# A per-token factor turned by VectorE and DMA instead of TensorE, in a Strassen-Winograd matmul chain

## The chip, the cores and the metric

The kernel runs on one core of a Trainium2 chip. The metric is the device time of one execution in microseconds (us). The engines of the core are TensorE (PE, with its weight loads listed apart as PEld), VectorE (DVE), ScalarE (ACT), GpSimd (POOL) and SyncE (SP, which here only issues DMAs). Everything is fp32.

## The reference, cut to what matters

x holds 8 batch rows of 256 tokens with 1024 features. Two layers follow each other, each added to its own input:

```
logits = x @ Wr.T + 5 * onehot(language of the row)          # 8 experts
w      = softmax(top 2 of logits);  gates = w at those two, 0 elsewhere
h      = x @ A.T                                              # 8 experts x 16 ranks = 128 numbers a token
x1     = x + x @ W.T + 2 * sum_e gates[e] * (h[e] @ B[e].T)   # W is 1024 x 1024
out    = x1 + x1 @ weight[adapter of the row].T               # 1024 x 1024, one of 16 by row
```

So per token there is a vector of 128 gated numbers, `gates * h`, and the last term of x1 is that vector times a 128 x 1024 matrix ("up projection").

## The kernel before, in words

**Layout.** Features lie on partitions, tokens along the free axis. The 2048 tokens are two halves j of 1024 and four quarters of 512. The product x @ W is done by Strassen-Winograd: seven products of 512 x 512 x 1024 blocks in place of eight, and most of these have two or three "leaves" that are split into seven again. The second layer (`adapt`, lines 896 to 1006) does the same per batch row with the row's weight; it comes after and takes from 226 us to the end.

**The first layer's order** is written out in lines 1031 to 1096: `opening` (product "1", mixed with the down projection of half 0), then the down projection of half 1 (`project`, lines 1037 and 1043), then `product` "2", "5", "6", "3", "7", "4". Products 2, 5, 3 and 4 also carry the up projection: `mm` (line 549) appends, after a block's own matmuls, one step per output half `ms` with `up[rows]` as stationary and `hg[tokens]` as moving operand (line 554). A step is two matmul instructions of 512 columns; four products with four such pairs of steps give 64 instructions. Product 2 and 4 read half 0 (`hg[0]`), 5 and 3 half 1.

**The gated numbers.** `project` leaves h and the logits in PSUM with tokens on partitions. `take` (line 265) adds the bias to the logits on DVE and copies h to `hT[j]` (128 tokens x 8 chunks x 128) on ACT. `gating(j)` (line 290) is a list of 20 small DVE operations (one on ACT), and at its end `onto_h`, which multiplies `hT[j]` by the gates (128 x 1024). The up projection needs the 128 numbers on partitions and tokens along the free axis, so `turn(j, banks)` (line 323) does 8 transposes of 128 x 128 on TensorE against the identity, and two ACT copies into `hg[j]`; the copy for j = 1 also changes the sign. `turn(0)` is called at line 1046, between the last `project` and product 2; `turn(1)` inside product 2 at its line 761 (`between`).

**What sets the order.** Each engine runs its instructions in program order; PE's order is written by hand. DVE's order is made at build time by a planner: it keeps a running time for PE and DVE (`now`), costs each DVE operation at (columns + 66)/960 us, and holds optional operations in `queue` as (cost, events to wait for, key, function). Before each DVE operation that empties a PSUM bank (`after`, line 394), `ahead` (line 366) issues from the queue what is ready and fits before PE gets there; `force(key)` (line 383) issues what PE is about to need. The chip itself waits by semaphores only. So an operation that is later than the planner thought delays what stands behind it on DVE, and PE where it needs that.

**Around the change.** Product 2 (line 693 on, key "2", leaves 2 and 4) starts with a block product into bank A, then ACT copies A to bank X (line 720), then come leaf 2's first piece into `single0` ("P" in the profile), block B5 (`t1`, `s1`) with its up step, leaf 2's piece 5 into `single1`, and a second block product that accumulates onto A. `single0` and `single1` hold the last down projection until `take(1, 1)` has emptied them; A must have been copied to X. On POOL's queue, `add_x` (line 1017) adds x blocks with DMAs into "12" and "22": those are inputs of products 5 and 6. On SP's queue, `raw("21", 0, 1)` (line 1065) follows product 2.

Of the kernel before, what the change touches and what calls it, by code (L numbers as in the profile page):

```python
# [9 lines left out]
F32 = mybir.dt.float32  # L10
I32 = mybir.dt.int32
AF = mybir.ActivationFunctionType
ALU = mybir.AluOpType
# [3 lines left out]
P = 128  # L17
NE = 8
LANG_BIAS = 5.0
SCALING = 2.0  # L20
# [5 lines left out]
def kernel(  # L26
# [62 lines left out]
    def flat(blk):  # L89
        return blk.rearrange("p k n -> p (k n)")  # L90
# [32 lines left out]

    aw_sb = flat(yb["12"])[:, : KC * EA].rearrange("p (k e) -> p k e", k=KC)
    hT = [flat(yb["22"])[:, j * C * ER : (j + 1) * C * ER].rearrange("p (c e) -> p c e", c=C) for j in range(2)]

    small = {}

# [92 lines left out]
    def copy(out_, x, scale=1.0):  # L221
        if scale == 1.0:
            nc.scalar.copy(out_, x)
        else:
            nc.scalar.activation(out_, x, AF.Copy, scale=scale)  # L225
# [13 lines left out]
        add(d, d, ident.unsqueeze(1).to_broadcast([P, k1 - k0, P]))  # L239


    hg = [const.tile([ER, 2, TQ], F32, name=f"hg{j}") for j in range(2)]
    lg = [rtile([P, C, E], f"lg{j}") for j in range(2)]
    gate8 = {}

# [43 lines left out]

    def gating(j):  # L290

        m1, hot1, ops1 = first_max(lg[j], j, 1)
        rest = rtile([P, C, E], "rest")
        m2, hot2, ops2 = first_max(rest, j, 2)
        dm = rtile([P, C], "dm")
        ex = rtile([P, C], "ex")
        den = rtile([P, C], "den")
        g1 = rtile([P, C], "g1")
        g2 = rtile([P, C], "g2")
        wide = [P, C, E]  # L300

        def onto_h():
            h = hT[j].rearrange("p c (e r) -> p (c e) r", r=R)
            g = hot1.rearrange("p c e -> p (c e)").unsqueeze(2).to_broadcast([P, C * E, R])
            tt(h, h, g, ALU.mult)


        ops = ops1 + [
            lambda: nc.vector.scalar_tensor_tensor(rest, hot1, NEG, lg[j], ALU.mult, ALU.add)
        ] + ops2 + [  # L310
            lambda: minus(dm, m2, m1),
            lambda: nc.scalar.activation(ex, dm, AF.Exp),
            lambda: nc.vector.tensor_scalar(den, ex, 1.0, None, ALU.add),
            lambda: nc.vector.reciprocal(g1, den),
            lambda: nc.vector.tensor_scalar(g1, g1, SCALING, None, ALU.mult),
            lambda: tt(g2, g1, ex, ALU.mult),
            lambda: tt(hot1, hot1, g1.unsqueeze(2).to_broadcast(wide), ALU.mult),
            lambda: tt(hot2, hot2, g2.unsqueeze(2).to_broadcast(wide), ALU.mult),
            lambda: add(hot1, hot1, hot2),
        ]  # L320
        return [(0.26, f) for f in ops] + [(us(2 * TQ), onto_h)]

    def turn(j, banks):

        for n in range(C):
            nc.tensor.transpose(banks[n // CQ][:, ts(n % CQ, P)], hT[j][:, n, :], ident)  # L326
        for c, ps_g in enumerate(banks):
            copy(hg[j][:, c, :], ps_g, -1.0 if j else 1.0)


    bdiff = const.tile([ER, OG + 3 * OQ], F32, name="bdiff")
# [19 lines left out]
    def us(n):  # L351
        return (n + 66) / 960

    def vec(t, fn, key=None):
        fn()
        now["dve"] += t
        done[key] = now["dve"] + 0.1

    def event(name, later=0.0):
        events[name] = now["pe"] + later  # L360
# [56 lines left out]
    def third(key, leaf, lhs, rhs, place, what):  # L417

        ra = lambda i, j: lhs()[:, j, ts(i, P)]
        rb = lambda i, j: rhs()[:, i, ts(j, NQ)]
        n0, n1 = slice(0, NQ), slice(NQ, TQ)
        t, own = {}, {}
        at = {"r13": 0, "r2": P, "r4": 2 * P, "q13": 3 * P, "q2": 3 * P + NQ, "q4": 3 * P + 2 * NQ}
        me = f"{key}:L{leaf}"

        def op(name, tag, fn, x, y, what):
            width = P if name[0] == "r" else NQ

            def run():
                if place == 0:
                    t[name] = sub3.tile([P, width], F32, name=f"{name}_{key}{leaf}", tag=tag)
                elif place == 3:
                    t[name] = flat(yb["12"])[:, 2048 + at[tag] : 2048 + at[tag] + width]
                else:
                    t[name] = spare(1536 + (place - 1) * 1152 + at[tag], width)
                fn(t[name], *(t[v] if isinstance(v, str) else v() for v in (x, y)))

            return us(width), what, f"{me}.{name}", run  # L440

        A, B = (lambda i, j: lambda: ra(i, j)), (lambda i, j: lambda: rb(i, j))
        ops = [
            op("r1", "r13", add, A(1, 0), A(1, 1), what),
            op("q1", "q13", minus, B(0, 1), B(0, 0), what),
            op("r2", "r2", minus, "r1", A(0, 0), what),
            op("q2", "q2", minus, B(1, 1), "q1", what),
            op("r4", "r4", minus, A(0, 1), "r2", what),
            op("q4", "q4", minus, B(1, 0), "q2", what),
        ]  # L450
        ops3 = [
            op("r3", "r13", minus, A(0, 0), A(1, 0), (f"{me}.5",)),
            op("q3", "q13", minus, B(1, 1), B(0, 1), (f"{me}.5",)),
        ]

        def piece(n, acc=None, banks=None, fresh=False):
            if n in (1, 5):
                own[n] = (single(f"P{n}_{key}{leaf}", n // 5) if banks is None else banks[n // 5])[:, n0]
            for x in {3: ("r4",), 4: ("q4",), 5: ("r1", "q1"), 6: ("r2", "q2", "P1"), 7: ("r3", "q3", "P6")}.get(n, ()):
                force(f"{me}.{x}")  # L460
            out_, l, r = {
                1: lambda: (own[1], ra(0, 0), rb(0, 0)),
                2: lambda: (acc[:, 0, n0], ra(0, 1), rb(1, 0)),
                3: lambda: (acc[:, 0, n1], t["r4"], rb(1, 1)),
                4: lambda: (acc[:, 1, n0], ra(1, 1), t["q4"]),
                5: lambda: (own[5], t["r1"], t["q1"]),
                6: lambda: (own[1], t["r2"], t["q2"]),
                7: lambda: (own[1], t["r3"], t["q3"]),
            }[n]()
            nc.tensor.matmul(out_, lhsT=l, rhs=r, start=(n in (1, 5) or fresh and n in (2, 4)), stop=True, skip_group_check=True)  # L470
            now["pe"] += 0.432
            event(f"{me}.{n}", 0.2)

        def take(n, dest, base=None, sub=False):

            cut = lambda v: {1: v[:, 0, n0], 6: v[:, 0, n1], 5: v[:, :, n1]}[n]
            if n == 7:
                cut = lambda v: v[:, 1, :].rearrange("p (j n) -> p j n", j=2)
            src = own[5 if n == 5 else 1]
            if n in (5, 7):  # L480
                src = src.unsqueeze(1).to_broadcast([P, 2, NQ])
            evict(NQ if n in (1, 6) else TQ, cut(dest), src, None if base is None else cut(base), f"{me}.P{n}", sub)

        return ops, ops3, piece, take
# [61 lines left out]
    def multiply(up=None, tokens=None):  # L546


        def mm(acc, lhs, rhs, first=False, rows=None, c=0, part=(0, 1), ms=(0, 1), need=()):
# [1 line left out]
                force(key)  # L551
            steps = [(lhs[:, k, ts(m, P)], rhs[:, k, :], m) for k in part for m in ms] if part else []
            if up is not None and rows is not None:
                steps += [(up[rows][:, ts(m, P)], hg[tokens][:, c, :], m) for m in ms]
            for i, (l, r, m) in enumerate(steps):
                nc.tensor.matmul(  # L556
                    acc[:, m, :],
# [132 lines left out]
        out(5, q2, q2)  # L690
        add(q2, A, q2)

    def product(key, base, dest, lora=None, tokens=None, sub=False, joined=None, between=None):

# [16 lines left out]
        own = list(deep[2][1]) if 2 in deep else []  # L713
        own += late[:1] + (deep[3][0] if 3 in deep else []) + late[1:] + (deep[4][0] if 4 in deep else [])
        own += (deep[3][1] if 3 in deep else []) + (deep[4][1] if 4 in deep else [])
        queue[:0] = own
        A = new("A")
        mm(A, a(0, 0), b(0, 0), True)
        X = new("X")
        nc.scalar.copy(X, A)  # L720
        if 2 in deep:
            _, _, piece, take = deep[2]
            piece(1)
            take(1, at[0], old[0], sub)
            B = new("B")
            mm(B, t["s1"], t["t1"], True, "1", 1, ms=(0,), need=K("s1", "t1"))
            piece(5)
            mm(A, t["s2"], t["t2"], need=K("s2", "t2"))
            event(f"{key}:P6", 0.2)
# [1 line left out]
            piece(6)  # L731
            take(6, at[0], old[0], sub)
            mm(B, t["s1"], t["t1"], True, "1", 1, ms=(1,))
            put(3, B, name="B5")
            for n in (2, 3, 4):
                piece(n, X)
# [19 lines left out]
        if 4 in deep:  # L756
            _, _, piece4, take4 = deep[4]
            piece4(1)
            take4(1, at[2], old[2], sub)
        if between is not None:  # L760
            between(X)
        if 3 in deep:
            hold[0] = key
            _, _, piece, take = deep[3]
# [278 lines left out]
    project(1, 1, singles("ps_h_1_1"))  # L1043
    now["pe"] += 7.5
    force("gates0")
    turn(0, halves(pair("ps_g_0", 2)))
    after(0.4, lambda: take(1, 1))
    now["pe"] += 1.8
    for k in (0, 2):
        add_x("12", "11", k, k + 2)  # L1050
    event("T1", 17.0)
# [1 line left out]
        add_x("22", "12", k, k + 2)  # L1053
    event("T2", 30.0)
    queue += [(t, (), f"gate{i}", f) for i, (t, f) in enumerate(gating(1))]
    gates = queue[-1][2]
    queue += make_subs("5", "21", "12", (2, 3, 4), ("T1",), "2", 1)

    def turn_1(X):
        force(gates)  # L1060
        turn(1, halves(X))
        now["pe"] += 1.8

    product("2", y21, y11, 0, 0, between=turn_1)
    raw("21", 0, 1)
    add_raw("21", 1, 1)
    event("T3", 30.0)
# [21 lines left out]
        y0[:] = y0 or prep_y(0)  # L1089
        y0[i][2]()  # L1090

    queue += [(0.6, ("4:P7", "7:join2"), f"4.y{i}", lambda i=i: prep_y0(i)) for i in range(4)]
    product("4", y21, y21, 1, 0)
    for q in list(queue):
        q[3]()
# [58 lines left out]
```

## Time and profile before

| | before |
|---|---|
| median of three runs (lowest to highest) | 424.62 us (424.34 to 425.0) |
| the profiled execution: own time, span | 424.31 us, 422.2 us |
| busy PE / PEld | 417.1 us (99%) / 230.7 us (55%) |
| busy DVE / ACT / POOL | 304.8 us (72%) / 40.9 us (10%) / 17.6 us (4%) |
| DMA queue of SP, share of 16 engines' span | 38.4% |
| DMA queue of POOL, share of 16 engines' span | 16.5% |
| granted TensorE clock | 1.00 |

The span runs from the first to the last instruction; the time of an execution has about 2.1 us more around it. "Busy" is the time in which an engine had an instruction in work. "A <- B" in a wait means that A stood still until B was done. In a timeline row the first number is the start, the second the length, both in us, and the bracket tells how long the engine stood idle just before.

### The profile page before, as it was taken

The numbers are of one execution on the slowest core, as the hardware profiler recorded it, in microseconds if no ns is written. First come the engines' busy times: TensorE is split into PE (matmuls) and PEld (weight loads), VectorE is DVE, ScalarE is ACT, GpSimd is POOL, SyncE is SP. The second block draws the span as 40 slices with busy tenths as digits, with TensorE's granted clock in tenths as the row PEclk, the third lists the DMA queues.
The fourth block names the chain that finished last, engine by engine and source line by source line (L and its number), as shares of the span: only waits on it lengthen the run. The fifth ranks groups of instructions, "written<-read, shape, count | busy, mean of one in ns | idle before, by whom it ended". The sixth has DMA issues, their size and how long they took to land.

```text
span 422.2 us, 3674 instructions
## 1 busy us (share of the span) xinstructions
PE 417.1 (99%) x1318; PEld 230.7 (55%) x1318; DVE 304.8 (72%) x489; ACT 40.9 (10%) x73; POOL 17.6 (4%) x26
## 2 busy tenths in 40 slices
PE   8999999999999999999999999999999999999996
PEld 6679975555655554554555444444444444444574
DVE  1977879968789999978799565765657666665531
ACT  2020130112110000000000101010101101010110
POOL 1000020110001101103000000000000000000000
PEclk9999999999999999999999999999999999999999
DMA  8995099576220946928903483765558384640202
GB/s 273 384 397 245 0 186 199 127 186 101 99 99 8 166 140 165 262 57 165 332 0 102 150 313 134 263 224 211 199 201 296 113 307 178 229 170 2 99 0 99
DMA packets 20257, 72.61 MB, mean 172 GB/s; under 512 B 1552, under 2 KB 3856, under 8 KB 15248
## 3 DMA queue, kind: packets, MB, share of 16 engines
q1 hardware_dynamic: 15088, 58.87, 38.4%
q0 software_dynamic: 3904, 12.58, 16.5%
q10 hardware_dynamic: 1248, 0.93, 0.7%
q8 instruction: 10, 0.16, 0.2%
q14 instruction: 7, 0.06, 0.1%
HBM read 55.61 MB, written 8.39 MB: 152 GB/s over the span
## 4 chain that ended last, share of the span: by engine, by line
PE 99%; POOL 0%; ACT 0%; issue 0%; POOLq 0%
PE A L908 23%; PE A L556 20%; PE B L908 13%; PE B L556 11%; PE ps_h L256 7%; PE X L908 7%; PE P L470 6%; PE A_last L975 3%; PE X L470 3%; PE X L556 3%; PE A L470 2%; PE B L470 1%; PE idle L573 1%; PE X L326 0%; PE ps_g L326 0%; ACT z L1005 0%
## 5 line engine op out<-in xcount | busy, mean ns | idle before, releaser
L556 PE MATMUL A<-t,s 128*128 128x512 f32 x112 | 50.3, 592 | 0.0
L908 PE MATMUL B<-x,x 128*128 128x512 f32 x96 | 43.2, 592 | 0.0
L228 DVE TENSOR_TENSOR w<-w,w 128x1024 f32<-128x1024 f32 x24 | 29.0, 1223 | 15.1 <-PE A L908 15.1
L908 PE MATMUL A<-w,x 128*128 128x512 f32 x88 | 39.6, 592 | 0.0
L908 PE MATMUL A<-w,y 128*128 128x512 f32 x88 | 39.1, 592 | 0.0
L256 PEld LDWEIGHTS ps_h<-y,x 128*128 128x128 f32 x256 | 31.7, 190 | 2.9 <-issue 2.4
L556 PEld LDWEIGHTS A<-t,s 128*128 128x128 f32 x112 | 21.2, 190 | 20.8 <-issue 20.1
L256 PE MATMUL ps_h<-y,x 128*128 128x136 f32 x256 | 31.9, 279 | 0.0
L908 PEld LDWEIGHTS B<-x,x 128*128 128x128 f32 x96 | 18.2, 190 | 22.1 <-issue 21.8
L228 DVE TENSOR_TENSOR y<-A,y 128x1024 f32<-128x1024 f32 x18 | 22.0, 1222 | 9.3 <-PE A L556 5.8
L908 PEld LDWEIGHTS A<-w,x 128*128 128x128 f32 x88 | 16.7, 190 | 21.0 <-issue 21.0
L908 PEld LDWEIGHTS A<-w,y 128*128 128x128 f32 x88 | 16.7, 190 | 20.6 <-issue 20.6
L228 DVE TENSOR_TENSOR y<-P,y 128x512 f32<-128x512 f32 (+1 forms) x37 | 21.1, 572 | 8.0 <-PE P L470 6.2
L556 PE MATMUL A<-x,w 128*128 128x512 f32 x56 | 25.3, 592 | 0.0
L228 DVE TENSOR_TENSOR x<-w,x 128x1024 f32<-128x1024 f32 (+1 forms) x12 | 10.9, 911 | 10.8 <-PE A L908 7.8
L228 DVE TENSOR_TENSOR w<-x,w 128x1024 f32<-128x1024 f32 x8 | 9.7, 1225 | 10.2 <-PE A L908 5.6
L225 ACT ACTIVATE z<-A 128x512 f32<-128x512 f32 x12 | 7.2, 597 | 101.0 <-PE A L908 101.0
L228 DVE TENSOR_TENSOR z<-z,X 128x512 f32<-128x512 f32 x7 | 4.8, 687 | 15.9 <-PE X L908 15.9
L556 PEld LDWEIGHTS A<-x,w 128*128 128x128 f32 x56 | 10.4, 190 | 10.3 <-issue 10.0
L556 PE MATMUL B<-x,s 128*128 128x512 f32 x32 | 14.9, 592 | 0.0
L228 DVE TENSOR_TENSOR x<-x 128x1024 f32<-128x1024 f32 (+1 forms) x15 | 14.7, 1005 | 0.0
L720 ACT COPY X<-A 128x1024 f32<-128x1024 f32 x6 | 6.0, 997 | 89.8 <-PE A L556 89.8
(203 smaller groups left out, 591.6 us busy)
## 6 DMA issues: line engine op xcount, KB each, us to landing
x<-w_dram SPq DMA_DIRECT2D x24, 1024.0 KB, 5.5
x<-xT_dram SPq DMA_DIRECT2D x10, 1024.0 KB, 11.0
w<-w_dram SPq DMA_DIRECT2D x8, 1024.0 KB, 4.7
out_dram<-z SPq DMA_DIRECT2D x15, 512.0 KB, 3.0
x<-x POOLq DMA_DIRECT2D x4, 1024.0 KB, 9.9
x<-xT_dram POOLq DMA_DIRECT2D x4, 1024.0 KB, 9.1
y<-y POOLq DMA_DIRECT2D x8, 512.0 KB, 5.1
w<-wT_dram SPq DMA_DIRECT2D x3, 1024.0 KB, 15.1
```

The costliest lines, as they stand in the source:

```text
L225: nc.scalar.activation(out_, x, AF.Copy, scale=scale)
L228: nc.vector.tensor_tensor(out_, x, y, op)
L256: nc.tensor.matmul(ps[v][:, u * EA : (u + 1) * EA], lhsT=xk(k, j, c)[:, ts(r, P)], rhs=aw_sb[:, k, :], start=(first and k == some[0] and u ...
L470: nc.tensor.matmul(out_, lhsT=l, rhs=r, start=(n in (1, 5) or fresh and n in (2, 4)), stop=True, skip_group_check=True)
L556: nc.tensor.matmul(acc[:, m, :], lhsT=l, rhs=r, start=(first and i < len(ms)), stop=(i >= len(steps) - len(ms)), skip_group_check=True,)
L573: nc.tensor.matmul(idle[:, 0, :P], lhsT=ident, rhs=ident, start=True, stop=True)
L720: nc.scalar.copy(X, A)
L908: nc.tensor.matmul(accs[name], lhsT=lhs[:, k // 2, k % 2, :], rhs=rhs[:, k, :], start=(first and k == 0), stop=(k == KH - 1), skip_group_c ...
L975: nc.tensor.matmul(acc, lhsT=lhs[:, k // 2, k % 2, :], rhs=rhs[:, k, ts(v, m)], start=(first and k == 0), stop=(k == KH - 1), skip_group_c ...
```

## The change

`turn(j)` no longer uses TensorE, PSUM or ACT. One DVE instruction turns every 32 x 32 square of `hT[j]` within its group of 32 partitions, into a scratch tile `squares[j]` (128 x 1024, in the quarter of y22 that product 5 writes later). Then each of the 4 x 4 groups of squares goes to its own partitions of `hg[j]`: twelve to other partitions by a DMA from SP (32 partitions x 1 KB each), the four on the diagonal by a GpSimd copy (32 x 256 numbers). `hg[j]` now holds for a number the tokens as (a, chunk, 32), so the up projection's moving operand is read by `turned` in 16 runs of 32 columns in place of one run of 512. The sign for j = 1 moves into a factor of the gates.

`turn` becomes the last entry of `gating(j)`: for half 0 it follows `onto_h` at once, for half 1 it waits in the planner's queue without a `force`. A small GpSimd copy `landed` reads all of `hg[0]`'s parts ahead of the first `add_x`. In product 2, B5's first half comes before leaf 2's first piece, and in products 2 and 5 its up step comes after B5's second half. Three planner rules change: a queue entry of the coming product keeps its place ahead of that product's own list; r3 and q3 wait also for r2 and q2; the four sums of the second layer's first row wait for leaf 3's piece 7 of product 4.

```diff
+    QS = P // 4
+    squares = [flat(yb["22"])[:, (2 + j) * C * ER : (3 + j) * C * ER] for j in range(2)]
...
-    hg = [const.tile([ER, 2, TQ], F32, name=f"hg{j}") for j in range(2)]
+    hg = [const.tile([ER, 4, C, QS], F32, name=f"hg{j}") for j in range(2)]
...
-            lambda: nc.vector.tensor_scalar(g1, g1, SCALING, None, ALU.mult),
+            lambda: nc.vector.tensor_scalar(g1, g1, -SCALING if j else SCALING, None, ALU.mult),
...
-        return [(0.26, f) for f in ops] + [(us(2 * TQ), onto_h)]
-
-    def turn(j, banks):
-        for n in range(C):
-            nc.tensor.transpose(banks[n // CQ][:, ts(n % CQ, P)], hT[j][:, n, :], ident)
-        for c, ps_g in enumerate(banks):
-            copy(hg[j][:, c, :], ps_g, -1.0 if j else 1.0)
+        return [(0.26, f) for f in ops] + [(us(2 * TQ), onto_h), (us(2 * TQ), lambda: turn(j))]
+
+    def turn(j):
+        nc.vector.transpose(squares[j], hT[j].rearrange("p n (b r) -> p b n r", b=4))
+        v = squares[j].rearrange("p (b n) -> p b n", b=4)
+        for a in range(4):
+            for b in range(4):
+                to = hg[j][b * QS : (b + 1) * QS, a].rearrange("p n q -> p (n q)")
+                if a != b:
+                    nc.sync.dma_start(to, v[a * QS : (a + 1) * QS, b])
+                else:
+                    nc.gpsimd.tensor_copy(to, v[a * QS : (a + 1) * QS, b])
+
+    def turned(j, c):
+        return hg[j][:, :, c * CQ : (c + 1) * CQ, :].rearrange("p a n q -> p n a q")
...
-        done[key] = now["dve"] + 0.1
+        done[key] = events[key] = now["dve"] + 0.1
...
-            op("r3", "r13", minus, A(0, 0), A(1, 0), (f"{me}.5",)),
-            op("q3", "q13", minus, B(1, 1), B(0, 1), (f"{me}.5",)),
+            op("r3", "r13", minus, A(0, 0), A(1, 0), (f"{me}.5", f"{me}.r2")),
+            op("q3", "q13", minus, B(1, 1), B(0, 1), (f"{me}.5", f"{me}.q2")),
...
-                steps += [(up[rows][:, ts(m, P)], hg[tokens][:, c, :], m) for m in ms]
+                steps += [(up[rows][:, ts(m, P)], turned(tokens, c), m) for m in ms]
...
-        queue[:0] = own
+        rest = list(queue)
+        queue[:] = [q for q in rest if q[2].startswith(key)] + own + [q for q in rest if not q[2].startswith(key)]
...
+            B = new("B")
+            if key == "2":
+                mm(B, t["s1"], t["t1"], True, ms=(0,), need=K("s1", "t1"))
             piece(1)
             take(1, at[0], old[0], sub)
-            B = new("B")
-            mm(B, t["s1"], t["t1"], True, "1", 1, ms=(0,), need=K("s1", "t1"))
+            up_late = key in ("2", "5")
+            if key != "2":
+                mm(B, t["s1"], t["t1"], True, None if up_late else "1", 1, ms=(0,), need=K("s1", "t1"))
             piece(5)
...
             mm(B, t["s1"], t["t1"], True, "1", 1, ms=(1,))
+            if up_late:
+                mm(B, None, None, False, "1", 1, part=(), ms=(0,))
...
-        if between is not None:
-            between(X)
...
     force("gates0")
-    turn(0, halves(pair("ps_g_0", 2)))
     after(0.4, lambda: take(1, 1))
-    now["pe"] += 1.8
+    landed = const.tile([ER, 4], F32, name="landed")
+    nc.gpsimd.tensor_copy(landed, hg[0][:, :, 0, 0])
...
-    def turn_1(X):
-        force(gates)
-        turn(1, halves(X))
-        now["pe"] += 1.8
-    product("2", y21, y11, 0, 0, between=turn_1)
+    product("2", y21, y11, 0, 0)
...
-    queue += [(0.6, ("4:P7", "7:join2"), f"4.y{i}", lambda i=i: prep_y0(i)) for i in range(4)]
+    queue += [(0.6, ("4:L3.7", "7:join2"), f"4.y{i}", lambda i=i: prep_y0(i)) for i in range(4)]
```

More of the change, by code (lines that the diff above doesn't have):

```diff
@@ L691, in opening, with product @@
         add(q2, A, q2)
-    def product(key, base, dest, lora=None, tokens=None, sub=False, joined=None, between=None):
+    def product(key, base, dest, lora=None, tokens=None, sub=False, joined=None):
         a, b, t, late, deep = subs.pop(key)
@@ L1055 @@
     queue += [(t, (), f"gate{i}", f) for i, (t, f) in enumerate(gating(1))]
-    gates = queue[-1][2]
     queue += make_subs("5", "21", "12", (2, 3, 4), ("T1",), "2", 1)
-    def turn_1(X):
-        force(gates)
-        turn(1, halves(X))
-        now["pe"] += 1.8
-    product("2", y21, y11, 0, 0, between=turn_1)
+    product("2", y21, y11, 0, 0)
     raw("21", 0, 1)
```

## The prediction

> **What bounds the kernel now.** I read the page's busy shares by slice first (columns: 40 slices of 10.6 us, tenths busy).
>
> ```profile
> PE   8999999999999999999999999999999999999996
> DVE  1977879968789999978799565765657666665531
> ```
>
> PE is full from end to end. The chain that ended last, in order of time, says the same more sharply (start, length, work, instructions):
>
> ```profile
> 43.29 14.83 PE ps_h L256 x128
> 58.11 0.87 PE ps_g L326 x8
> 58.99 3.44 PE A L556 x8
> 62.42 0.43 PE P L470 x2
> 62.85 2.58 PE B L556 x6
> 65.43 0.43 PE P L470 x2
> 65.86 3.43 PE A L556 x8
> ...
> 79.18 0.43 PE P L470 x2
> 79.61 0.87 PE X L326 x8
> 80.48 2.58 PE B L556 x6
> ```
>
> Each piece begins where the one before it ends: PE waits for nothing here. So every us of PE work taken away is a us off the end, and every wait put before PE is a us on it; nothing else counts. The two L326 pieces are the transposes. What PE needs from the others around the first of them is in the timelines of DVE and ACT:
>
> ```profile
> 51.73 1.22 DVE L228 TENSOR_TENSOR y<-y,y 128x1024 f32<-128x1024 f32 x1
> ...
> 60.40 0.25 DVE L228 TENSOR_TENSOR y<-ps_h,bias 128x16 f32<-128x16 f32 x2
> ...
> 62.89 0.42 DVE L228 TENSOR_TENSOR y<-P,y 128x256 f32<-128x256 f32 x1 [1.73 <-PE P L470]
> ```
>
> ```profile
> 59.02 1.07 ACT L223 COPY hg<-ps_g 128x512 f32<-128x512 f32 x2 [3.22 <-PE ps_g L326]
> 60.60 0.65 ACT L273 COPY y<-ps_h 128x256 f32<-128x256 f32 x2 [0.50 <-DVE y L228]
> 62.46 1.00 ACT L720 COPY X<-A 128x1024 f32<-128x1024 f32 x1 [1.22 <-PE A L556]
> ```
>
> 51.73 is onto_h. DVE then runs without idle to take(1,1) at 60.40. ACT's copies of take(1,1) follow, then A to X, done at 63.46; PE's second block product into A starts at 65.86.
>
> **Removed.** 2 x 8 transposes: 2 x 0.87 = 1.74 us of PE, all on the path, and four ACT copies (0.59 each), off it. A rule speaks against the change: the Trainium skill ("VectorE: DVE Perf Modes", The three transpose paths and Rules for kernel authors) sends a 128 x 128 transpose to TensorE, at 390 ns (its table is bf16), because VectorE turns only squares of 32. By its figure 16 of them would be 6.2 us; the row has 0.109 us each in a run. I take the row: the gain is 1.74.
>
> **Added on DVE, half 0.** One transpose of 1024 columns behind onto_h. No row has one. Nearest: the 1024-column operation, 1.22 us, the next one starting 1.15 after it. Low end 1.15; high end twice, 2.3, if fp32 goes at half rate; below 1.15 there is no reason, as no one-source 1024-column row shows it. I take 1.15. It delays all of DVE up to take(1,1) by d.
>
> Where d meets PE: ACT's copies end at 61.25 + d, A to X at 62.25 + d. PE in the new order, from 58.11: A 3.44 to 61.55, B5's first half without its up step 1.72 to 63.27, piece 1 to 63.70, piece 5 to 64.13, second product into A. The wait is therefore d - 1.88 if positive. Piece 1 needs single0, emptied by about 60.93 + d: 2.34 of room; had B5's half not been moved ahead of it, 0.62 only, and 0.5 lost. With d = 1.15 nothing waits; with 2.3, 0.4.
>
> **Added on POOL.** Four copies of 32 x 256 per half. No row has a copy; the affine select of 128 columns on ident took 0.28 and a memset of one column 0.10, so by (0.28 - 0.10)/128 a column some 0.46 us each, 1.84 for four. The skill ("SBUF — State Buffer", SBUF: two separate sides) says a GpSimd operation and a VectorE one with two SBUF inputs exclude each other for the whole instruction. Between 54 and 60 DVE runs just such operations (s, t, r, q). By the rule d is up to 1.15 + 1.84 = 2.99, and PE waits 1.1. The rows show no such loss: POOL's DMA work at 52.86 to 53.77 lay beside DVE's s and t, which took their usual 0.68 and 1.22; but that is not a copy, so the row is only near. I take zero in the likeliest case and keep 1.1 for the range.
>
> **Added on SP.** Twelve issues per half. Plain issues took 0.33 to 0.38 each: 4.0 to 4.5 us. Half 0: from 54.0, last issue at 58.5, landed 1.9 later (the 128 KB store) or 5 if busy: 60.4 to 63.5. The first up step in the new order is at 69.7 (64.13 + 3.43 + 0.43 + 1.72): 6 us of cover or more. SP has nothing else then.
>
> Behind `landed`, POOL's first add_x slips from 52.86 to about 61 (64 at the late end). Before, the blocks had landed by 66.88, when POOL's next wait ended; then by 75 to 78. DVE reads that block at 78.97; nothing lost, or a few tenths on DVE. The next add_x pair lands by 86 to 89, is read at 100.39.
>
> **Half 1.** The transpose is unforced, at best right behind the gates (DVE at 69); following the planner's costs by hand I get about 83, behind leaf 4's sums. SP's twelve issues then end by 89 and land by 94. The first use of hg[1] is the up step behind B5's second half in product 5: 102.23 - 1.74 = 100.5. Moved past on SP: raw("21"), issued at 73.19 before, slips by some 15; on POOL its add_raw (80.83, 92.89) likewise. The block is read by product 7's sums, after 149. Behind the wait on POOL stand only those. DVE's load in product 2: its idle stretches from 61 to 90 were 1.73 + 0.31 + 0.29 + 0.42 + 1.24 = 3.99; against that 1.15 (or 2.3) more work, 0.87 less time and up to 1.84 from POOL's copies: 3.86, just inside. Past 92.6 another 4.2 us are idle.
>
> **Moved for nothing.** The up steps and B5's half are the same matmuls in another order. The sign rides in an existing operation. The planner's three rules shift DVE work only: what is queued for a product is needed some us later. The four sums ran at 219.10 and 222.17; now behind leaf 3's piece 7 (222.57 - 1.74), the first done by about 224 and needed at 227.7. If that cover failed, 0.6 a sum.
>
> **The moving operand.** 64 instructions now read 16 runs of 32 columns. No row of a strided moving operand exists. All contiguous ones stream a 512-column instruction each 0.429 us, 0.84 ns a column. DVE's sums over y in runs of 128 took the same 0.685 as contiguous ones; the nearest row says 0. Above: c column times per run cost 64 x 16 x 0.84 ns x c = 0.86 c us. Below zero is excluded: no instruction can beat its own column count. I take 0.
>
> Sum: 424.31 - 1.74 = 422.57 for the profiled execution; the median is 0.31 above that execution, so 422.9.
>
> **Rivals.**
> 1. *Likeliest (0.60)*: all cover holds, 422.9; own range 422.5 to 423.2.
> 2. *DVE arrives late in product 2 (0.22)*: the transpose or POOL's copies push d past 1.88, and PE stands before the second product into A (or later in product 2). 0.1 to 1.1 lost, middle 0.6: 423.5. For it: the skill's lock, and a chain with 0.73 of room. Against: POOL and DVE rows side by side.
> 3. *The strided operand costs (0.10)*: from two column times per run the gain is gone; with four, 3.4 - 1.7 = 1.7 us slower, 426.3. For it: no row. Against: the operand's runs are long, 128 bytes each. About 0.06 of it ends slower, the rest in between.
> 4. *The change doesn't do what it says, a transfer or sum is late (0.08)*: hg lands behind 69.7 or 100.5, or product 5's blocks come late by the slipped add_x; 1 to 2 lost, 423.9 to 424.9.
>
> **How the numbers follow.** A measurement tells about 0.2% (0.85 us) from no change: faster means below 423.77. Case 1 whole, most of case 2 (0.18), a little of 3 and 4 (0.03): 0.81. Within: 0.04 + 0.02 + 0.06 = 0.12. Slower: 0.06 and 0.01 = 0.07. Range 422.4 to 424.0: cases 1 and 2 and the near part of 4.
>
> **What the profile after would show.** Right: no L326 rows, PE busy down 1.7, the chain without a gap at 64 and 70; hg steps still 592 ns; DVE's transpose near 1.2. Wrong: PE idle before A at 64 (released by ACT X) is case 2, with lengthened DVE operations from 54 to 60 if it is the lock; hg steps over 592 ns or spaced over 0.429 is case 3; PE idle behind a DMA into hg, or DVE behind x<-x, is case 4.

## The result

| | before | after |
|---|---|---|
| median (lowest to highest) | 424.5 us (424.1 to 425.0), 8 runs | 423.13 us (422.5 to 423.6), 8 runs |
| ratio | | 0.9966, 95% interval 0.9955 to 0.9977 |
| profiled execution: own time, span | 424.31, 422.2 | 422.77, 421.0 |
| busy PE / DVE / ACT / POOL | 417.1 / 304.8 / 40.9 / 17.6 | 415.5 / 308.0 / 38.6 / 24.1 |

The change takes 1.4 us off, where 1.74 was forecast; 423.13 lies in the forecast range of 422.4 to 424.0.

The profile after, busy tenths by slice:

```profile
PE   8999999999999999999999999999999999999996
DVE  1977888999788999978789676665657566765531
```

VectorE is fuller from 84 to 105 us: 9 and 9 tenths, where it had 6 and 8. The chain that ended last, over the stretch that was shown for before and at its last piece on DVE:

```profile
43.28 14.83 PE ps_h L259 x128
58.10 3.43 PE A L569 x8
61.54 1.72 PE B L569 x4
63.25 0.86 PE P L483 x4
...
109.42 1.57 DVE y L230 x2
```

There are no transposes, and the order A, B, P is there as the prediction had it, to 0.02 us. Then the chain leaves PE: from 78.34 to 111.03 it runs through DVE, which before it never did. PE's own timeline shows where the two meet (start, length, instruction):

```profile
109.08 1.88 PE L569 MATMUL B<-hg,bdiff 128*128 128x512 f32 x4
111.03 0.70 PE L483 MATMUL X<-x 128*128 128x256 f32 x2
111.57 0.59 PE L483 MATMUL P<-x 128*128 128x256 f32 x2
```

A row's successor begins 0.16 before the row's end when nothing is waited for. The second row should begin at 110.80; it begins at 111.03 and is 0.11 longer, so 0.34 is lost. It is leaf 3's piece 5 in product 5. PE's weight loads say for whom they waited, and DVE's rows why that came when it did:

```profile
111.03 0.30 PEld L483 LDWEIGHTS X<-x 128*128 128x128 f32 x2 [0.91 <-DVE y L230]
```

```profile
107.16 1.23 DVE L230 TENSOR_TENSOR y<-X,y 128x1024 f32<-128x1024 f32 x1
108.30 0.28 DVE L230 TENSOR_TENSOR r<-w 128x128 f32<-128x128 f32 x1
...
109.42 1.22 DVE L230 TENSOR_TENSOR y<-A,y 128x1024 f32<-128x1024 f32 x1
110.56 0.41 DVE L230 TENSOR_TENSOR y<-X,y 128x256 f32<-128x256 f32 x1
```

The 110.56 row is `take(1)` of leaf 3, which empties the bank of its first piece; the load starts as it ends. It stands behind the eviction of bank X (107.16), four sums for product 6 (rows r and q, 1.1 us together) and the eviction of bank A (109.42). Before, the same load waited for the same operation too, but just in time:

```profile
111.75 0.42 DVE L228 TENSOR_TENSOR y<-X,y 128x256 f32<-128x256 f32 x1
112.23 0.51 PEld L470 LDWEIGHTS X<-x 128*128 128x128 f32 x2 [0.34 <-DVE y L228]
112.55 0.59 PE L470 MATMUL X<-x 128*128 128x256 f32 x2
```

PE's row of 112.55 begins 0.16 before the end of the one ahead of it (110.83 and 1.88 long), as scheduled. The room there was nearly nil, and no row of PE shows it, since PE did not stand still.

Measured from the start of the last down projection (43.29 before) to the start of the last matmul row (414.91 before), which leaves out the jitter of the opening, the execution is 371.62 before and 370.22 after: 1.40 less, that is 1.74 - 0.34. The experiments below call this "the stretch".

### The profile page after: what moved, and what is told of

The parts are those of the page before. It is cut to its first block, busy times and chain, and to the rows that moved or that the text cites. A ratio compares the mean times of both kernels' runs of the same rounds, so it can differ in the third digit from the quotient of the medians.

```text
span 421.0 us, 3695 instructions
## 1 busy us (share of the span) xinstructions
PE 415.5 (99%) x1302; PEld 228.7 (54%) x1302; DVE 308.0 (73%) x491; ACT 38.6 (9%) x69; POOL 24.1 (6%) x35
## 4 chain that ended last, share of the span: by engine, by line
PE 91%; DVE 7%; issue 1%; POOL 0%; ACT 0%; DVEq 0%; POOLq 0%
PE A L926 23%; PE A L569 17%; PE B L926 13%; PE B L569 9%; PE ps_h L259 7%; PE X L926 7%; PE P L483 5%; PE A_last L993 3%; DVE y L230 3%; PE X L483 2%; PE X L569 2%; PE A L483 2%; DVE t L230 1%; PE B L483 1%; DVE x L230 1%
```

## The experiments

**1. The diagonal copies on ScalarE.**

```diff
-                    nc.gpsimd.tensor_copy(to, v[a * QS : (a + 1) * QS, b])
+                    nc.scalar.copy(to, v[a * QS : (a + 1) * QS, b])
```

> The four diagonal copies of each half move from GpSimd to ScalarE; all else as in the changed kernel. Theory (0.34 us of the gain is lost in product 5, where TensorE waits for VectorE, which has been behind since the two transposes and GpSimd's copies): VectorE's operations beside the copies shrink back from 1.42 to 1.22 us, it reaches take(1) of leaf 3 in product 5 some 0.6 to 1.0 earlier, the wait at 111 us goes, 422.8. Rival (the copies don't matter, the lost 0.34 is elsewhere): the long operations stay at 1.42 or the wait stays, 423.1.

Measured: 422.54 us, before 424.36 on the same chip, ratio 0.9956 (0.9943 to 0.9969). The stretch is 369.87: 1.75 under before, and PE has no gap. GpSimd's copies and DVE's operations beside them, in the changed kernel:

```profile
54.29 3.41 POOL L338 COPY hg<-y 32x256 f32<-32x256 f32 x4 [51.48 <-DVE y L330]
```

```profile
54.72 1.42 DVE L230 TENSOR_TENSOR t<-x 128x1024 f32<-128x1024 f32 x1
...
57.35 1.42 DVE L230 TENSOR_TENSOR t<-x,t 128x1024 f32<-128x1024 f32 x1
```

and with the copies on ScalarE:

```profile
55.67 1.21 DVE L230 TENSOR_TENSOR t<-x 128x1024 f32<-128x1024 f32 x1
...
58.09 1.22 DVE L230 TENSOR_TENSOR t<-x,t 128x1024 f32<-128x1024 f32 x1
```

The two t rows shrink from 1.42 to 1.22. The copies cost DVE 0.2 for each operation that meets one: 0.4 in half 0, some 0.6 in half 1 (82.9 to 85.8). That is enough for the wait. The intervals of this kernel's ratio and of the changed kernel's overlap, so the verdict on 0.34 us rests on the stretch and the missing gap, not on the medians.

**2. The hold of product 5 begins earlier.** While `hold` names a product, `ahead` issues from the queue only what belongs to that product.

```diff
+        if key == "5":
+            hold[0] = key
         put(3, A, True, "A7")
```

> Only the planner's hold of product 5 starts before the eviction of A7, so that the four r and q operations of product 6 (1.1 us) no longer stand ahead of A7 and take(1). Theory: take(1) comes 1.1 earlier, the wait at 111 us goes, 422.8 with no other change; leaf 2 of product 6 gets its r and q at about 121, needed at 123.3. Rival (the missing 0.34 is not this wait, or the wait only moves into product 6): 423.1 or slower.

Measured: 422.58 us, ratio 0.9955 (0.9942 to 0.9968); the stretch is again 369.87, and PE:

```profile
108.91 1.88 PE L569 MATMUL B<-hg,bdiff 128*128 128x512 f32 x4
110.63 0.59 PE L483 MATMUL X<-x 128*128 128x256 f32 x2
```

There is no gap, and none in product 6. DVE's work is the same and only its order differs; so the lost 0.34 was this one wait, and what stood ahead of `take(1)` decided it.

**3. The edits of 1 and 2 together.**

> Both cures at once: diagonal copies on ScalarE and the earlier hold in product 5. Theory (one wait of 0.34 was all that was lost; each cure removes it): no more than either alone, 422.6, TensorE without a gap from 43 us on, which is 1.74 under the kernel before. Rival (GpSimd's lock costs something beyond that wait): 0.2 or more below 422.5.

Measured: 422.51 us against 424.65, ratio 0.9954 (0.9941 to 0.9966); the stretch is 369.87 once more. Each cure removes the same wait, and both together win no more than either. What is left is PE's own work.

**4. Each transpose issued twice.**

```diff
-        nc.vector.transpose(squares[j], hT[j].rearrange("p n (b r) -> p b n r", b=4))
+        for _ in range(2):
+            nc.vector.transpose(squares[j], hT[j].rearrange("p n (b r) -> p b n r", b=4))
```

> Each transpose on VectorE is issued twice (1.17 more per half). Theory with the 1.88 threshold: d goes from 1.64 to 2.8, TensorE waits 0.9 before the second product into A of product 2; the second one adds its whole 1.17 to the wait in product 5, since VectorE has no idle time between: 2.1 slower than the changed kernel, 425.2. Rival (there is idle time enough on VectorE up to product 5, the threshold is wrong): under 0.5 slower, 423.1 to 423.6.

Measured: 425.76 us, ratio 1.003 (1.0018 to 1.0041), some 2.7 over the changed kernel by the ratios and 2.6 by the stretch. PE's gaps:

```profile
64.28 0.70 PE L484 MATMUL P<-x,w 128*128 128x256 f32 x2 [0.70 <-ACT y L276]
...
94.56 1.99 PE L570 MATMUL B<-x 128*128 128x512 f32 x4 [0.89 <-DVE y L230]
...
113.93 0.70 PE L484 MATMUL X<-x 128*128 128x256 f32 x2 [0.18 <-DVE y L230]
```

d, the delay of take(1,1), was 2.93 (from onto_h's start to take(1,1)'s, 11.60 in place of 8.67). By the starts of PE's rows 0.86 were lost before the first of these, another 0.23 before the second product into A, and 0.10 more behind each of the two waits, where a row is longer because its weight load was not hidden: 1.29 in all, where d - 1.88 gives 1.05. The second half's 1.17 did not go where I expected: 1.05, and 0.10 behind it, are lost at product 5's first B block, which has to wait for the eviction of product 2's last block (y<-A,y, 93.28 to 94.50; the block starts at 94.56). In the changed kernel that row ends at 91.62 and the block begins at 91.89: 0.27 of room, 0.99 before. At 113.93 0.44 are lost, 0.10 more than in the changed kernel. Together that is 2.5 more than there, where 2.1 was expected: the place was wrong for the second part, and the first part was mis-sized.

**5. B5's first half back behind leaf 2's first piece.**

```diff
-            if key == "2":
-                mm(B, t["s1"], t["t1"], True, ms=(0,), need=K("s1", "t1"))
...
-            if key != "2":
+            if True:
                 mm(B, t["s1"], t["t1"], True, None if up_late else "1", 1, ms=(0,), need=K("s1", "t1"))
```

> In product 2 B5's first half goes back behind leaf 2's first piece (its up step stays late). Theory: the first piece is then due at 61.54 but single0 is emptied only at 62.6, TensorE waits about 1.05 there; VectorE gains that much room, so the 0.34 in product 5 goes: 423.8 (423.8 to 424.2). Rival (single0 is free in time and the move covers nothing): 423.1.

Measured: 424.43 us, ratio 1.000 (0.9992 to 1.0009): the whole gain is gone. PE:

```profile
63.26 0.70 PE L483 MATMUL P<-x,w 128*128 128x256 f32 x2 [1.13 <-ACT y L276]
```

1.29 are lost before this row and 0.10 behind it for the exposed weight load (1.05 expected), so the move does cover a wait. The wait at product 5 stayed too (0.33), against my expectation: between 63 us and 75 DVE stands still three times for PE's own results (1.44, 0.69 and 0.68 in the changed kernel), so a later PE gives DVE no lead for what comes behind.

**6. Half 1 turned by TensorE, at its old place.**

```diff
-        return [(0.26, f) for f in ops] + [(us(2 * TQ), onto_h), (us(2 * TQ), lambda: turn(j))]
+        return [(0.26, f) for f in ops] + [(us(2 * TQ), onto_h)] + ([] if j else [(us(2 * TQ), lambda: turn(j))])
...
+    def turn_pe(j, banks):
+        for n in range(C):
+            nc.tensor.transpose(banks[n // CQ][:, ts(n % CQ, P)], hT[j][:, n, :], ident)
+        for c, ps_g in enumerate(banks):
+            copy(turned(j, c), ps_g.rearrange("p (n a q) -> p n a q", n=4, a=4))
...
+        if between is not None:
+            between(X)
         if 3 in deep:
...
+    def turn_1(X):
+        force(gates)
+        turn_pe(1, halves(X))
+        now["pe"] += 0.9
...
```

> Half 1 is turned by TensorE again, at its old place in product 2, with copies by ScalarE into the new layout; half 0 as in the changed kernel. Theory (each half is worth its 0.87 us of TensorE, and only half 1's transpose, copies and later gates fill VectorE up to the wait in product 5): 0.87 under the kernel before, 423.5, no wait at 111 us. Rival (half 0's transpose is what sets VectorE back): the wait of 0.3 stays, 423.8.

Measured: 428.53 us, ratio 1.0092 (1.0074 to 1.0110). Both theories failed. PE:

```profile
82.48 1.97 PE L342 MATMUL X<-ident,y 128*128 128x128 f32 x8 [3.00 <-DVE y L230]
84.24 2.59 PE L575 MATMUL B<-x,s 128*128 128x512 f32 x4
```

The gates of half 1 now come late on DVE: the last seven gate operations and onto_h stand behind the eviction of leaf 2's last piece (75.65), onto_h at 81.20 in place of 67.82. By the code, the planner's clock for DVE is 1.1 further on by half 0's transpose and its clock for PE 1.8 back; that this moved them is read from the code, no run tests it. A TensorE transpose due at 79 us waits 3.2 us for onto_h. In the changed kernel onto_h is as late, but no PE instruction waits for it then. Besides, after the gap the same instructions are slow (the two rows were 1.04 and 1.88 before): the granted clock was 0.50 from 82.3 to 85.6 and 1.00 again from 85.7 on, and 1.6 more were lost.

**7. The same, the transposes behind B3's eviction.** The edit against experiment 6:

```diff
-        if between is not None:
-            between(X)
         if 3 in deep:
...
         put(1, B, True, "B3")
         join(1)
+        if between is not None:
+            between(X)
```

> As half1_pe, but TensorE's eight transposes of half 1 stand later in product 2, behind block B3's eviction, where the gated numbers have long been ready. Theory (the loss of half1_pe was its wait for the gates, and the slower clock behind that wait; each half is worth 0.87 us, and without half 1's transpose and GpSimd copies VectorE is in time in product 5): no wait in products 2 and 5, 0.87 under the kernel before, 423.6. Rival (half 0's part alone sets VectorE back): a wait of 0.3 at 111 us, 423.9.

Measured: 423.41 us against 424.39, ratio 0.9973 (0.9965 to 0.9982); the stretch is 370.75, 0.87 under before; no gap. So one half is worth its 0.87, and half 0's transpose and copies alone make PE wait nowhere.

**8. Without `landed`.**

```diff
-    landed = const.tile([ER, 4], F32, name="landed")
-    nc.gpsimd.tensor_copy(landed, hg[0][:, :, 0, 0])
```

> The small GpSimd copy that makes the add_x transfers wait for hg[0] is left out. Theory (hg[0] has 5 us of cover up to 69.5 us): add_x issues at about 58 in place of 64.5, hg[0] lands a few us later beside it but before 69.5, no change, 423.1. Rival (the large transfers hold the small ones back past 69.5): TensorE waits before the first up step of product 2, 1 us or more slower.

Measured: 430.9 us against 424.65, ratio 1.0152 (1.0138 to 1.0167): the rival holds. PE at its first up step:

```profile
75.24 3.64 PE L569 MATMUL B<-hg,b_sb 128*128 128x512 f32 x4 [4.68 <-issue]
```

add_x was issued at 58.50 in place of 64.45, beside the small transfers into hg[0]. From then on SP's issues of those took 1.14 to 1.46 each, and their landing 7.1 to 9.3 us; with `landed`, most issues took 0.59 and no landing of half 0 more than 3.2. The row's wait is put to "issue", that is to nothing the view names, but the trace has its cause: the last of the twelve transfers, issued at 65.8, took 9.1 us, to 74.9, and PE goes on at 75.24. PE lost 4.8 us there, and the row took 3.64 for four instructions that usually take 1.88: the granted clock was 0.50 from 75.4 to 78.7 and 1.00 again from 78.8 on.

## Why the prediction was right, and by how much it was not

- **The gain is PE's own work**: right. Free of waits the stretch is 1.75 shorter (experiments 1 to 3), where 1.74 were summed, and one half is worth 0.87 (experiment 7). It went by the trace's row, not by the 390 ns that the Trainium skill ("VectorE: DVE Perf Modes", The three transpose paths) gives for one transpose.
- **DVE's transpose 1.15**: right; 1.25 long, the next operation 1.17 later.
- **The room of 1.88 in product 2**: there, but smaller, and nearly used up. d was forecast at 1.15 and came to 1.65. Nothing waited, yet the weight load of the second product into A came 0.1 late, since it waited for ACT's copy of A to X (62.77 to 63.80), and PE's row at 63.95 was just in time:

```profile
63.85 0.30 PEld L569 LDWEIGHTS A<-t,s 128*128 128x128 f32 x2
```

  With d at 2.93 that product began 1.19 late, so the room is 1.74; and piece 1, with 2.34 reckoned, lost 0.86 and not 0.59. The sums also left out the 0.10 of an exposed weight load behind each wait. That no wait appeared here was partly luck.
- **POOL's copies, 0.46 each and no loss to DVE**: wrong. A copy took 0.39 at best and 1.30 at worst, and DVE lost 0.4 and some 0.6. The Trainium skill's rule ("SBUF — State Buffer", SBUF: two separate sides), that of two such operations the later one waits for the whole of the other, fits these rows: the copy that starts at 55.10 beside DVE's t row of 54.72 ends at 56.40, after that row, and the next one (56.44), which meets none, takes 0.40. What went wrong with the bound of 1.84 is that it laid the whole length of all copies on DVE, three to five times what was lost there; most of the waiting fell on the copies. My row of a POOL DMA beside DVE was no guide for a copy.
- **SP's issues, 0.35 each**: mis-sized, 0.59 in the middle and up to 1.36; hg[0] was there at 63.9, past my 63.5. The cover up to 69.5 held only because `landed` kept the large transfers back. I priced what `landed` delays and never what would happen without it.
- **add_x's slip** (blocks landed by 75 to 78): right, POOL's waits ended at 72.02 and 77.09. **Half 1's transpose at 83**: it came at 81.71. **raw("21")**: it slipped by 18.5, where I had 15, and nobody waited.
- **The strided operand at zero**: right. Up steps are 592 ns and 0.429 apart as before, in X, A and B.
- **The four sums**: the first was done at 223.38 (224 forecast).
- **DVE's load**: this step failed. The prediction had "3.86, just inside" of 3.99, and "past 92.6 another 4.2 us are idle": the count ended at 90 us and took the 4.2 as a reserve. Here is the busy time from the eviction of leaf 2's last piece in product 2 to leaf 3 of product 5, before and after (columns: window, its length, then busy PE, PEld, DVE, ACT, POOL, the granted clock, DMA share, GB/s):

```profile
75.78:112.00 36.22, 36.22 (x107) 19.45 (x106) 30.43 (x51) 5.63 (x9) 2.58 (x2) 1.00 0.58 139
```

```profile
74.90:111.00 36.10, 36.05 (x100) 18.62 (x98) 35.53 (x63) 4.55 (x7) 6.37 (x7) 1.00 0.84 192
```

  DVE has 5.1 us more work in the same time, and its two idle stretches there (1.24 and 4.20) are gone. Besides the transpose (1.17) and the copies (0.6), 2.8 us of gates and onto_h had moved in from ahead of this window, and three r and q operations of product 6 (0.9); these are reckoned from start to start, so the short gaps between operations are in them. The reserve was spent, and idle time ahead of the window could not be used for it. The moved order is also a term that the prediction put at nothing ("Moved for nothing": the planner's rules "shift DVE work only"): experiment 2 changes the order alone, and the wait goes. Which edit moved the gates and the sums, the three rules or the planner's clocks, stays open. In the prediction's terms it is rival 2, at its low end and one product later. 423.13 also lies in the likeliest case's own range of 422.5 to 423.2, though that case's mechanism (all cover holds) failed; that is luck, and only the trace tells the two apart.

The sum's error is one term of 0.34, put at zero.

## What to carry to other kernels

Where one engine is full from end to end, moving work off it is worth that work only as long as each of its weight loads and bank reuses still finds its producer in time: look in the trace of before for producers that end within a few tenths of a us of the load they release, since these waits are invisible until they cost something. Count a second engine's load not in sum but from one forced wait to the next, since idle time ahead of such a wait can't be spent behind it. And a small transfer on the path must be kept clear of large ones that are queued beside it: here that order is worth 6.6 us by the stretch (experiment 8 against the changed kernel), slower clock included.

## What the runs showed of the hardware

- A GpSimd copy of 32 x 256 numbers and a VectorE operation with two SBUF inputs hinder each other: the VectorE operation of 1.22 us took 1.42, and the copies took 0.39 to 1.30. With the copies on ScalarE it took 1.22.
- A long PE gap costs more than itself. Behind gaps of 3.2 and 4.8 us (experiments 6 and 8) the granted clock was 0.50 for over 3.3 us, and 1.6 to 1.8 us more were lost; behind gaps of about 1 us (experiments 4 and 5) it stayed at 1.00, and only the 0.1 of an exposed weight load was lost.
- Of twelve transfers of 32 KB, the six that were issued beside large ones of 1 MB took 1.14 to 1.46 us each to issue and 7.1 to 9.3 us to land (experiment 8); kept ahead of the large ones, the twelve took mostly 0.59 to issue and 3.2 at most to land.
- A moving operand in 16 runs of 32 fp32 columns streams like one run of 512: 0.592 us an instruction and 0.429 from one to the next in both.
- One VectorE transpose of 128 x 1024 fp32 in squares of 32 takes as long as an addition of that size: 1.25 against 1.22 us.
